# Attention with an adjacency bias: projections in quarters over all steps, checks in the last groups, first loads from two engines

## The chip, the cores and the metric

One Trainium2 chip, one of its cores. The time is device microseconds for one execution of the kernel, the median of several runs; lower is better. The core has a matrix engine (PE), a vector engine (DVE), a scalar engine that does the exponentials (ACT), a general engine (POOL) and a queue engine (SP) that here issues nearly all transfers.

## The reference

The input is `x` (2708 nodes, 128 features), an adjacency matrix `adj` (2708 x 2708, float32), and the weights of two layers. Layer 0 is attention over all pairs of nodes, for 128 "heads" `d` that have 8 features each:

```python
q = (x @ Wq.T).reshape(d, n, h)          # d = 128, n = 2708, h = 8; k and v alike
a = jnp.einsum('dnh,dmh->dnm', q, k) * scale
a = jax.nn.softmax(a + adj + adj, axis=2)
out = jnp.einsum('dnm,dmh->dnh', a, v).reshape(n, h * d) @ Wo.T
x = layernorm(x + out)
```

Layer 1 is two products with `adj`, small weight products and another layernorm. Nearly all the work is in layer 0: 128 x 2708 x 2708 scores, an exponential of each, and the weighted sums.

## The kernel before, in words

**Tiling.** Heads go in 32 groups of four (GB). In a group, queries go in six blocks of 452 (QB; the last has 448), keys in 21 chunks of 128 nodes and a short one of 20. For a block of queries, the pairs (chunk, head) make pieces of two, and one `interleave` step holds two to four pieces: 9 steps per block, 54 per group, 1728 in all. The plan of nine steps is the same for all blocks.

**What a step does.** For each piece, PE multiplies keys and queries into one of two PSUM buffers `s` (`score`, L415), and DVE adds the adjacency columns to it and writes it to the step's tile `e` (`add_near`, L422). ACT then takes exp(2 x) of the whole tile (L518). Nine chunks, one per step (`TWO_EXP`), are treated in another way to relieve DVE: three of their four heads are scored into a PSUM tile `p`, ACT takes exp(2 p) (L515), and POOL multiplies by exp(2 adj) of that chunk (L516). Tiles of products (`w`) and of exponentials (`e`) go to the second product, `add_up` on PE (L440), as moving operands. ACT's order in a step is L515, then L518.

**exp(2 adj).** It is made in group 0, one tile `ecol` per step, by `first_exp` on ACT (L397), just ahead of L515, and stored to `near_exp` in device memory by SP (L398, `ne<-ecol`). Later groups load it. `look_at_near` (L404) reduces such a tile on DVE to a minimum or maximum per row; `rest` tests these, together with the sums, and if a limit is passed a second, slower attention runs. It doesn't run on these inputs.

**The projections.** q, k and v of the first two chunks of 128 rows of `x` are made at the start (L371 to L380), which is what group 0 needs. The other 20 chunks are cut into 120 halves of 512 columns (`halves`), in the order of chunk, then keys, queries, values, then half. A half is one matmul into an `s` buffer (L343), a scaling copy by DVE (L345) and *jobs*. For keys and queries these are a cast and a subtraction on POOL (L356, L357), which split the value into two parts, and a store (L352); for values a store (L347). The last job of each is the load of the next half's weights (`load_half`, L335). `proj` has one buffer for each tile. One job is popped per step, at its second piece:

```python
if c == 1 and jobs:
    jobs.pop(0)()
```

**What sets the order.** `interleave` is a planner: it holds assumed costs (`PROJECT`, `TAKE`, `SPLIT` for projections) and yields pieces, `add_up`s, `amid` (a projection, ahead of the first piece of a step named in `amid`) and `hand_on`. PE gets its instructions in that order, and every engine takes its own in order. SP's queue is in the order of the program too: at the head of a step query loads, key loads and value loads for the next group, adjacency loads eight ahead, then, in group 0, the store of exp(2 adj), and behind it, at the second piece, the job of that step.

**The start.** SP loads `x` and weights, eight adjacency tiles and the first weights of a half; PE, ACT and DVE make the first projections; SP stores keys and queries, loads the 16 parts of `k_raw` (L254) and the eight of `q` (L287), then stores and loads values. The casts of the keys (L262) on POOL, DVE and ACT need all 16 parts.

Of the kernel before, what the change touches and what calls it, by code (L numbers as in the profile page):

```python
# [9 lines left out]
F32 = mybir.dt.float32  # L10
F32R = mybir.dt.float32r
I32 = mybir.dt.int32
AF = mybir.ActivationFunctionType
ALU = mybir.AluOpType
AX = mybir.AxisListType
# [3 lines left out]
P = 128  # L19
H = 8  # L20
GB = 4
NB = 512
# [17 lines left out]
def interleave(plan, blocks, short, amid=(), bufs=4, patience=0.1):  # L40
# [9 lines left out]
    EXP, EXP_ADDED, EXP_TILE = 0.07, 0.14, 0.37  # L50
    PROJECT, TAKE, SPLIT = 0.95, 0.7, 1.25
    n_plan = len(plan)
# [11 lines left out]
    ready, summed, queue, sums, again = {}, {}, [], None, False  # L64
    n, c, left = 0, 0, None
    amid, seen = set(amid), 0
    while n < blocks * n_plan or queue:
# [3 lines left out]
        elif n < blocks * n_plan:  # L71
# [5 lines left out]
            if None not in old:  # L77
                at = added[-2] + HOP
                rows = [r for m, j in tiles for r in (range(GB) if m == short else [j])]
                beside = [j for j in left if j not in rows][:2] if banks + HOP <= max(pe, at) else []  # L80
                if c == len(pieces) - 1:
                    beside = list(left)
                    at = max(at, banks + HOP) if left else at
                starts.append((at, "piece"))
        if queue and not (queue[0][1] == first_chunk and sums is not None):
            qb, qm = queue[0]
            at = max([ready[p, qb * n_plan + k] for p, k in held[qm]] + [free_acc] * (qm == first_chunk)) + HOP
            starts.append((at, "add_up"))
        soon = [s for s in starts if s[0] <= pe + patience]
        at, what = soon[0] if soon else min(starts)  # L90
# [52 lines left out]
def graph_attention_gcn(ctx: ExitStack, tc: tile.TileContext, x, xT, adj, adjT, adjP, adjS,  # L143
# [10 lines left out]
    nc = tc.nc  # L154
# [34 lines left out]
    with ExitStack() as s:  # L189
# [57 lines left out]

        def load_keys(g, h):


            if h == 0:
                groups[g] = kpool.tile([P, NU, P], F32R, tag="k", name="k"), k_short[g % 2], vals[g % 2], v_short[g % 2]
                raw_keys[g] = raw.tile([P, N], F32R, tag="k_raw", name="k_raw")
            nc.sync.dma_start(raw_keys[g][ds(H * h, H), :].bitcast(F32),  # L254
                              ks[ds(H * (h % 4 // 2), H), ds((GB * g + h // 4) * N, N)])
# [25 lines left out]

        def load_q(g, b):
            n0, nw = QBS[b]
            q = queries[g, b] = qpool.tile([P, QB], F32R, tag="q", name="q")
            for j in range(GB):
                for i in range(2):
                    nc.sync.dma_start(q[ds(32 * j + 2 * H * i, 2 * H), :nw].bitcast(F32),  # L287
                                      qs[:, ds((GB * g + j) * N + n0, nw)])
# [31 lines left out]
        assert GB * N <= FIRST * P * P  # L320
        halves = [(c, i, h) for c in range(FIRST, NM) for i in range(3) for h in range(2)]
        given = {}
# [4 lines left out]

        def load_half(n):
            c, i, h = halves[n]
            i0, mi = MC[c]  # L330
            if i == h == 0:
                given[c] = proj.tile([P, P], F32, tag="xc", name="xc")
                nc.sync.dma_start(given[c][:, :mi], xT[:, ds(i0, mi)])
            given[c, i, h] = proj.tile([P, NB], F32, tag="wc", name="wc")
            nc.sync.dma_start(given[c, i, h], projections[i][0][:, ts(h, NB)])  # L335

        def project(n):

            c, i, h = halves[n]
            i0, mi = MC[c]  # L340
            dst = projections[i][1]
            pp = ps.tile([P, 2, NB], F32, tag="s", name="s")
            nc.tensor.matmul(pp[:mi, 0, :], given[c][:, :mi], given.pop((c, i, h)), start=True, stop=True)  # L343
            a = proj.tile([P, NB], F32, tag="pa", name="pa")[:mi]
            nc.vector.tensor_scalar_mul(a, pp[:mi, 0], half_scale if i == 1 else 1.0)  # L345
            if i == 2:
                return [lambda: nc.sync.dma_start(dst.rearrange("(i g) e -> i (g e)", g=P)[ds(i0, mi), ts(h, NB)], a)]  # L347
            o = proj.tile([P, 2, NB], F32R, tag="pr", name="pr")[:mi]

            def store():  # L350
                for l in range(2):
                    nc.sync.dma_start(dst.rearrange("r (i g) -> i r g", g=P)[ds(i0, mi), ds(H * l + 4 * h, 4)],  # L352
                                      o[:, l].bitcast(F32).rearrange("p (e g) -> p e g", g=P))


            return [lambda: nc.gpsimd.tensor_copy(o[:, 0], a),  # L356
                    lambda: nc.gpsimd.tensor_sub(o[:, 1], a, o[:, 0].bitcast(F32)), store]  # L357

# [5 lines left out]
        for n in range(ahead):  # L364
            load_adj(n)
        load_half(0)
        for i, (_, dst) in enumerate(projections):
            for c in range(FIRST):
                pp = ps.tile([P, 2, NB], F32, tag="s", name="s")
                for h in range(2):  # L370
                    nc.tensor.matmul(pp[:, h, :], first_x[:, ts(c, P)], first_w[:, ts(2 * i + h, NB)], start=True, stop=True)  # L371
                o = flat(epool.tile([P, 8, QB], F32, tag="e", name="e"))[:, : 4 * NB].rearrange("p (l f) -> p l f", l=2)
                if i == 2:
                    nc.scalar.copy(o[:, 0], flat(pp))
                    nc.sync.dma_start(dst.rearrange("(i g) e -> i (g e)", g=P)[ts(c, P)], o[:, 0])
                else:
                    f = half_scale if i == 1 else 1.0
                    nc.scalar.mul(o[:, 0].bitcast(F32R), flat(pp), f)
                    nc.vector.scalar_tensor_tensor(o[:, 1].bitcast(F32R), flat(pp), f, o[:, 0], ALU.mult, ALU.subtract)
                    nc.sync.dma_start(dst.rearrange("r (i g) -> i r g", g=P)[ts(c, P)],  # L380
                                      o.rearrange("p l (e g) -> p (l e) g", g=P))
            if i == 1:
                for h in range(16):
                    load_keys(0, h)
                load_q(0, 0)
        for j in range(GB):
# [6 lines left out]
        def first_exp(b, m):  # L393

            nw = QBS[b][1]
            t = ecols.tile([P, QB], F32, tag="ecol", name="ecol")
            nc.scalar.activation(t[:, :nw], adj_cols[0, b, -1 - m][:, :nw], AF.Exp, scale=2.0)  # L397
            nc.sync.dma_start(near_exp[b, m][:, :nw], t[:, :nw])  # L398
            exp_cols[0, b, m] = t

        def look_at_near(g, b, m):
            x = TWO_EXP.index(m)
            if g < 8 and g % 4 == x % 4:
                nc.vector.tensor_reduce(ends[:, g // 4, ds(b * len(TWO_EXP) + x, 1)], exp_cols[g, b, m][:, : QBS[b][1]],  # L404
                                        AX.X, (ALU.min, ALU.max)[g // 4])

# [44 lines left out]

        amid = list(range(2, 54, 6)) + [54 * g + t for g in range(1, NG) for t in (2, 10, 18, 26)]
        amid = amid[: len(halves)]
        for g in range(1, NG):
            c = (min(NG, g + 2) * GB * N - 1) // (P * P)
            assert c < FIRST or amid[halves.index((c, 2, 1))] + 8 < 54 * g
        jobs = []
        loaded = ahead
        for what, n, c, beside in interleave(plan, len(steps) // len(plan), NU, amid, bufs=5):
            if what == "amid":  # L460
                at = amid.index(n)
                jobs += project(at)
                if at + 1 < len(halves):
                    jobs.append(lambda n=at + 1: load_half(n))
                continue
# [368 lines left out]
```

## Time and profile before

| what | value |
|---|---|
| median of 3 runs | 6898.54 us (6897.92 to 6901.11) |
| the profiled execution | 6904.39 us, span of its instructions 6902.6 us |
| start to first exp of products (L515) | 48.7 us |
| group 0, 54 steps | 238.9 us |
| groups 1 to 7 | 202.7 to 208.3 us each |
| groups 8 to 27 | 201.7 to 202.1 us each |
| groups 28 to 31 | 201.2, 199.8, 200.2, 196.7 us |
| the rest (output projection, layer 1) | 346.4 us |
| granted PE clock, mean | 0.994 |

A stage's time is read from one group's first L515 to the next one's. In a row of busy times by stage the number after the window is its length, and for each engine the busy time and the instructions in it follow. In a row of a group of instructions the numbers after "x" are count, busy time, mean nanoseconds of one, and the idle time of the engine just before them with what ended it. In a timeline the first number is the start, the second the duration, and the bracket holds the idle time before and what ended it. Idle time of an engine matters only where ACT, or whatever sets the pace, waits for it.

### The profile page before, as it was taken

Reading aid. Unit: us, or ns where it says so; the run is one execution under the profiler, and the core shown is the slowest. Engines: PE = TensorE matmul, PEld = TensorE weight load, DVE = VectorE, ACT = ScalarE, POOL = GpSimd, SP = SyncE. Lnnn points to the kernel's source line nnn. Section 1 sums busy time; section 2 is a strip of 40 time slices with the busy share of each in tenths; the row PEclk is TensorE's granted clock in tenths of the full one; section 3 lists DMA queues with packets and bytes.
Section 4 is the critical chain, followed back from the end, with each engine's and each line's share of the span. In section 5 each row is a group of like instructions: output and inputs, shape, how many; then the busy total and the mean of one; then the engine's idle time right before and its main releaser. Section 6 shows DMA issues by size and latency. Waiting matters only on the chain.

```text
span 6902.6 us, 137500 instructions
## 1 busy us (share of the span) xinstructions
PE 6641.2 (96%) x50426; PEld 1983.7 (29%) x50426; DVE 6112.2 (89%) x6307; ACT 6501.8 (94%) x3605; POOL 5761.7 (83%) x2546
## 2 busy tenths in 40 slices
PE   7999999999999999999999999999999999999979
PEld 2222222222222222222222222222222222222254
DVE  6899999999999999999999999999999999999941
ACT  7999999999999999999999999999999999999910
POOL 5888888888888989888898988889898888888800
PEclk8999999999999999999999999999999999999999
DMA  8888887878888888888878788877888887777667
GB/s 266 269 246 243 249 239 234 246 241 242 249 245 243 243 246 245 253 246 247 241 242 249 245 251 248 248 240 243 244 244 255 247 240 232 231 235 239 199 203 232
DMA packets 1143258, 1674.16 MB, mean 243 GB/s; under 512 B 148922, under 2 KB 1090366, under 8 KB 1138478
## 3 DMA queue, kind: packets, MB, share of 16 engines
q1 hardware_dynamic: 1142574, 1665.29, 79.7%
q8 instruction: 399, 6.54, 0.4%
q14 instruction: 285, 2.33, 0.1%
HBM read 1582.90 MB, written 81.80 MB: 241 GB/s over the span
## 4 chain that ended last, share of the span: by engine, by line
PE 54%; DMA 13%; DVE 12%; POOL 8%; issue 6%; ACT 4%; SPq 3%; DVEq 0%; POOLq 0%; ACTq 0%
PE acc L440 27%; PE s L415 18%; DVE e L422 11%; POOL w L516 7%; DMA col<-in_adjP 4%; PE acc L661 3%; ACT w L515 2%; DMA k_raw<-ks 2%; PE p L415 2%; ACT e L518 2%; PE acc L437 2%; DMA two<-in_adjP 2%; DMA ecol<-ne 1%; PE s L343 1%; DMA q<-qs 1%
## 5 line engine op out<-in xcount | busy, mean ns | idle before, releaser
L516 POOL TENSOR_TENSOR w<-w,ecol 128x1356 f32<-128x1356 f32 (+1 forms) x1728 | 5347.4, 3102 | 755.0 <-ACT w L515 622.6
L422 DVE TENSOR_TENSOR e<-s,col 128x904 f32<-128x904 f32 (+1 forms) x4608 | 4831.3, 1092 | 339.9 <-PE s L415 196.8
L518 ACT ACTIVATE e<-e 128x2712 f32<-128x2712 f32 (+5 forms) x1728 | 4747.6, 2747 | 17.4 <-DVE e L422 14.8
L440 PE MATMUL acc<-e,vals 128*9 128x452 f32 x20352 | 3553.2, 545 | 0.1
L415 PE MATMUL s<-q,k 32*128 32x452 f32 x10944 | 2501.3, 462 | 183.4 <-DVE e L422 117.7
L515 ACT ACTIVATE w<-p 128x1356 f32<-128x1356 f32 (+1 forms) x1728 | 2439.2, 1412 | 47.1 <-PE p L415 28.5
L415 PEld LDWEIGHTS s<-q,k 32*128 32x128 f32 x10944 | 1016.7, 182 | 3370.6 <-DVE e L422 2979.4
L440 PE MATMUL acc<-w,vals 128*9 128x452 f32 x10368 | 1622.6, 545 | 0.0
L415 PE MATMUL p<-q,k 32*128 32x452 f32 (+1 forms) x5184 | 1400.5, 446 | 18.7 <-ACT w L515 18.4
L422 DVE TENSOR_TENSOR e<-s,two 128x904 f32<-128x904 f32 (+1 forms) x960 | 1049.1, 1093 | 119.9 <-PE s L415 61.1
L440 PEld LDWEIGHTS acc<-e,vals 128*9 128x9 f32 x20352 | 452.0, 89 | 807.7 <-issue 805.8
L415 PEld LDWEIGHTS p<-q,k 32*128 32x128 f32 x5184 | 575.5, 182 | 63.9 <-ACT w L515 53.6
L440 PEld LDWEIGHTS acc<-w,vals 128*9 128x9 f32 x10368 | 200.9, 88 | 193.2 <-issue 177.5
L262 POOL CAST k<-k_raw 128x336 fp32r<-128x336 f32 x251 | 222.3, 886 | 37.6 <-DMA q<-qs 37.6
L432 PE MATMUL acc<-e,v_short 128*128 128x452 f32 (+1 forms) x384 | 197.1, 595 | 0.0
L437 PE MATMUL acc<-e,v_first 128*32 128x452 f32 (+1 forms) x1536 | 185.9, 556 | 2.5
L343 PE MATMUL s<-wc,xc 128*128 128x512 f32 (+1 forms) x240 | 136.3, 650 | 6.4 <-DMA wc<-in_WvT 3.4
L345 DVE TENSOR_SCALAR pa<-s 128x512 f32<-128x512 f32 (+1 forms) x120 | 82.9, 691 | 48.6 <-PE s L343 46.2
L446 DVE COPY o<-acc 128x452 f32<-128x452 f32 x192 | 118.9, 619 | 6.4 <-PE acc L440 6.4
L661 PE MATMUL acc<-col,xw 128*128 128x512 f32 (+2 forms) x264 | 105.5, 549 | 0.0
L555 ACT ACTIVATE sd<-mv,eps 128x1 f32<-128x1 f32 (+1 forms) x22 | 6.0, 294 | 104.5 <-DVE mv L549 104.4
L661 PE MATMUL acc<-col,hw 128*128 128x512 f32 (+2 forms) x264 | 104.1, 545 | 0.0
(84 smaller groups left out, 1069.0 us busy)
## 6 DMA issues: line engine op xcount, KB each, us to landing
col<-in_adjP SPq DMA_DIRECT2D x1965, 226.0 KB
two<-in_adjP SPq DMA_DIRECT2D x1440, 226.0 KB
ecol<-ne SPq DMA_DIRECT2D x1395, 226.0 KB
col<-in_adjP SPq DMA_DIRECT2D x393, 224.0 KB
two<-in_adjP SPq DMA_DIRECT2D x288, 224.0 KB
ecol<-ne SPq DMA_DIRECT2D x279, 224.0 KB
col<-in_adjT SPq DMA_DIRECT2D x210, 256.0 KB
k_raw<-ks SPq DMA_DIRECT2D x512, 84.6 KB
```

The source lines that it names most:

```text
L262: copy(k[:, :, ts(i, n)], t[:, ts(i, n * NU)].rearrange("p (q c) -> p c q", c=NU))
L343: nc.tensor.matmul(pp[:mi, 0, :], given[c][:, :mi], given.pop((c, i, h)), start=True, stop=True)
L415: nc.tensor.matmul(to[:, :nw], k[r, m, :], q[r], start=True, stop=True)
L422: nc.vector.tensor_add(e[:, ds(at, 2), :nw], st[:, :, :nw], a)
L432: nc.tensor.matmul(a[:, :nw], vz, e[:, t, :nw], start=False, stop=False)
L437: nc.tensor.matmul(a[ds(32 * j, 32), :nw], v_first[g % 2][:, ds(32 * j, 32)], e[:, t, :nw], start=True, stop=False)
L440: nc.tensor.matmul(a[ds(32 * j, VW), :nw], v[:, m, ds(VW * j, VW)], e[:, t, :nw], start=False, stop=(m == last_chunk))
L446: nc.vector.tensor_copy(o[:, :nw], acc.pop((g, b))[:, :nw])
L515: nc.scalar.activation(w[:, :, :nw], sp[:, :, :nw], AF.Exp, scale=2.0)
L516: nc.gpsimd.tensor_mul(w[:, :, :nw], w[:, :, :nw], exp_cols[g, b, two][:, :nw].unsqueeze(1).to_broadcast([P, 3, nw]))
L518: nc.scalar.activation(e[:, :at, :nw], e[:, :at, :nw], AF.Exp, scale=2.0)
L661: nc.tensor.matmul(acc[:, :nw], src[:mw, m, :], t[:mw, :nw], start=(m == 0), stop=(last is None and m == NM - 1))
```

## The change

Three things change.

1. Projections are cut in quarters of 256 columns instead of halves of 512: 240 instead of 120. Before, the steps of `amid` were nine in group 0 (every sixth from 2) and four in each later group (2, 10, 18, 26) until they were used up in group 28. Now they are 18 in group 0 (every third from 2), and then every seventh step from 58 to 1605, in group 29. Cast and subtraction are one job, so that keys and queries have three jobs (split, store, load the next) and values two (store, load the next). The planner's costs of a projection are lowered.
2. The check of exp(2 adj): the maximum is replaced by the row sum that `first_exp` leaves as accumulator output, in group 0. The minimum is taken in groups 29 to 31, three of the nine chunks in each, instead of minima in groups 0 to 3 and maxima in groups 4 to 7: 54 reductions instead of 108.
3. At the start, query stores, every third part of the keys and half of the query parts are issued by ACT instead of SP. The loads of keys and queries are written after all first projections, and the value stores behind them, so SP's own order of these is as before.

```diff
-    PROJECT, TAKE, SPLIT = 0.95, 0.7, 1.25
+    PROJECT, TAKE, SPLIT = 0.5, 0.36, 1.0
...
-        halves = [(c, i, h) for c in range(FIRST, NM) for i in range(3) for h in range(2)]
+        quarters = [(c, i, h) for c in range(FIRST, NM) for i in range(3) for h in range(4)]
+        QW = 2 * P
...
-            nc.tensor.matmul(pp[:mi, 0, :], given[c][:, :mi], given.pop((c, i, h)), start=True, stop=True)
-            a = proj.tile([P, NB], F32, tag="pa", name="pa")[:mi]
-            nc.vector.tensor_scalar_mul(a, pp[:mi, 0], half_scale if i == 1 else 1.0)
+            nc.tensor.matmul(pp[:mi, 0, :QW], given[c][:, :mi], given.pop((c, i, h)), start=True, stop=True)
+            a = proj.tile([P, QW], F32, tag="pa", name="pa")[:mi]
+            nc.vector.tensor_scalar_mul(a, pp[:mi, 0, :QW], half_scale if i == 1 else 1.0)
+
+            def load():
+                if n + 1 < len(quarters):
+                    load_quarter(n + 1)
+
             if i == 2:
-                return [lambda: nc.sync.dma_start(dst.rearrange("(i g) e -> i (g e)", g=P)[ds(i0, mi), ts(h, NB)], a)]
+                to = dst.rearrange("(i g) e -> i (g e)", g=P)[ds(i0, mi), ts(h, QW)]
+                return [lambda: nc.sync.dma_start(to, a), load]
...
+            def split():
+
+                nc.gpsimd.tensor_copy(o[:, 0], a)
+                nc.gpsimd.tensor_sub(o[:, 1], a, o[:, 0].bitcast(F32))
...
-            return [lambda: nc.gpsimd.tensor_copy(o[:, 0], a),
-                    lambda: nc.gpsimd.tensor_sub(o[:, 1], a, o[:, 0].bitcast(F32)), store]
+            return [split, store, load]
...
-                    nc.sync.dma_start(dst.rearrange("r (i g) -> i r g", g=P)[ts(c, P)],
-                                      o.rearrange("p l (e g) -> p (l e) g", g=P))
-            if i == 1:
-                for h in range(16):
-                    load_keys(0, h)
-                load_q(0, 0)
+                if i == 2:
+                    made[c] = o
+                else:
+                    (nc.sync if i == 0 else nc.scalar).dma_start(dst.rearrange("r (i g) -> i r g", g=P)[ts(c, P)],
+                                                                 o.rearrange("p l (e g) -> p (l e) g", g=P))
+        for h in range(16):
+            load_keys(0, h, nc.scalar if h % 3 == 2 else nc.sync)
+        load_q(0, 0, (nc.sync, nc.scalar))
+        for c in range(FIRST):
+            nc.sync.dma_start(vs.rearrange("(i g) e -> i (g e)", g=P)[ts(c, P)], made[c][:, 0])
...
-            nc.scalar.activation(t[:, :nw], adj_cols[0, b, -1 - m][:, :nw], AF.Exp, scale=2.0)
+            x = b * len(TWO_EXP) + TWO_EXP.index(m)
+            nc.scalar.activation(t[:, :nw], adj_cols[0, b, -1 - m][:, :nw], AF.Exp, scale=2.0,
+                                 accum_out=ends[:, 1, x : x + 1])
...
-            if g < 8 and g % 4 == x % 4:
-                nc.vector.tensor_reduce(ends[:, g // 4, ds(b * len(TWO_EXP) + x, 1)], exp_cols[g, b, m][:, : QBS[b][1]],
-                                        AX.X, (ALU.min, ALU.max)[g // 4])
+            if x % 3 == g - NG + 3:
+                nc.vector.tensor_reduce(ends[:, 0, ds(b * len(TWO_EXP) + x, 1)], exp_cols[g, b, m][:, : QBS[b][1]],
+                                        AX.X, ALU.min)
...
-        amid = list(range(2, 54, 6)) + [54 * g + t for g in range(1, NG) for t in (2, 10, 18, 26)]
-        amid = amid[: len(halves)]
+        amid = list(range(2, 54, 3))
+        amid += range(58, 58 + 7 * (len(quarters) - len(amid)), 7)
...
                 jobs += project(at)
-                if at + 1 < len(halves):
-                    jobs.append(lambda n=at + 1: load_half(n))
```

## The prediction

> **What bounds the kernel now.** First the page's busy shares and its slices, then the busy time by stage with one stage per group of four heads, then the groups by form for prices, and last the timeline at the start and at one projection.
>
> ```profile
> PE 6641.2 (96%) x50426; PEld 1983.7 (29%) x50426; DVE 6112.2 (89%) x6307; ACT 6501.8 (94%) x3605; POOL 5761.7 (83%) x2546
> ```
>
> No engine stands out over the whole span, so I cut it. A stage runs from the first exp of products (L515 on ACT) of one group to that of the next, 54 steps:
>
> ```profile
> core 0: us, PE busy (x) PEld busy (x) DVE busy (x) ACT busy (x) POOL busy (x), PEclk, DMA share, GB/s
> 48.68:287.53 238.85, 212.83 (x1498) 59.06 (x1502) 199.15 (x208) 226.61 (x161) 188.30 (x92) 0.95 0.90 276
> 490.44:698.74 208.30, 198.84 (x1542) 55.73 (x1538) 191.67 (x197) 202.52 (x110) 181.10 (x81) 0.98 0.79 238
> 1109.43:1312.13 202.70, 198.26 (x1548) 56.33 (x1540) 192.09 (x198) 200.84 (x109) 180.64 (x81) 1.00 0.81 244
> 2125.71:2327.42 201.71, 197.85 (x1542) 56.11 (x1538) 186.06 (x185) 200.43 (x110) 179.21 (x79) 1.00 0.81 245
> 5959.52:6159.30 199.78, 192.99 (x1534) 57.44 (x1530) 182.02 (x180) 199.78 (x110) 175.26 (x75) 1.00 0.77 233
> ```
>
> In group 29 (last row), which has neither projections nor checks, ACT is busy for all of its 199.78 us: ACT sets the pace, and a step costs 3.7 us. Groups 8 to 27 have four half projections each and take 201.7 to 202.1: 1.7 us for four. Groups 1 to 7 have the same halves and 12 or 18 checks each, and take 1434.65 together, 22.6 more than seven times 201.72: 0.25 us for each of 90 checks. Group 0 takes 238.85: the floor of 199.8, plus 54 exps of the adjacency (L397) on ACT that lengthen a step by 0.47 each (25.4), plus about 13 of idle ACT. So the whole that can be won from projections and checks is their sum over the groups, some 80 us, and nothing that only frees DVE or PE wins unless ACT was waiting for it.
>
> ```profile
> L397 ACT ACTIVATE ecol<-col 128x452 f32<-128x452 f32 x45 | 26.2, 583 | 0.0
> L404 DVE TENSOR_REDUCE ends<-ecol 128x1 f32<-128x452 f32 x90 | 55.4, 616 | 6.2 <-ACT ecol L397 6.2
> L343 PE MATMUL s<-wc,xc 128*128 128x512 f32 x228 | 130.1, 653 | 6.4 <-DMA wc<-in_WvT 3.4 <-DMA wc<-in_WkT 2.2 <-DVE e L422 0.7
> L345 DVE TENSOR_SCALAR pa<-s 128x512 f32<-128x512 f32 x114 | 78.8, 691 | 47.4 <-PE s L343 45.6 <-POOL w L516 1.3
> ```
>
> The third row is the one to keep: the projection's matmul has already waited for its weights (wc), 3.4 and 2.2 us, both in group 0. The timeline shows what one such wait costs:
>
> ```profile
> 155.91 0.35 SPq L335 DMA_DIRECT2D wc<-in_WvT  x1
> 157.62 1.31 ACT L515 ACTIVATE w<-p 128x1356 f32<-128x1356 f32 x1
> ...
> 160.68 1.24 PE L343 MATMUL s<-wc,xc 128*128 128x512 f32 x2 [3.36 <-DMA wc<-in_WvT]
> 162.03 0.69 DVE L345 TENSOR_SCALAR pa<-s 128x512 f32<-128x512 f32 x1 [3.91 <-PE s L343]
> 167.67 1.30 ACT L515 ACTIVATE w<-p 128x1356 f32<-128x1356 f32 x1 [5.17 <-PE p L415]
> ```
>
> PE takes its work in order, so everything behind the projection waits too. ACT's L515 comes 10.05 us after the one before instead of about 4.7: 5.3 us lost by a 3.36 us wait. The rest is the clock: from 161.5 to 168.3 PEclk is 0.50 and score matmuls take about 740 ns instead of 470.
>
> At the start, the 16 key loads and 8 query loads set the first score:
>
> ```profile
> 20.97 13.79 SPq L254 DMA_DIRECT2D k_raw<-ks  x16
> 35.45 7.07 SPq L287 DMA_DIRECT2D q<-qs  x8
> 42.33 1.68 ACT L262 CAST k<-k_raw 128x336 fp32r<-128x336 f32 x2 [20.55 <-DMA q<-qs]
> ```
>
> **What the Trainium skill says.** "TensorE: Matmul & The Clock Gate", Part 1, has the array fall to half its clock after an idle window of about 3.4 us; the trace agrees, with half clock for 6.8 us after the wait of 3.36. "DMA: Bandwidth & Descriptors", Issuing engines are not separate DMA queues, says that transfers of all issuing engines interleave on the same 16 DMA engines and only issue time is saved; its section Why a DMA increments its semaphore by 16 and not by 1 says that a transfer of 8 partitions uses the lowest 8 of them. The trace agrees with the second: during the key loads (26.5 to 36 us) the DMA share is 0.51, at 89 GB/s, one load per 0.96 us. "ScalarE: Activation LUTs", What ACT_TABLE_LOAD costs, prices a ScalarE instruction at 186 ns plus 0.833 per element, with 93 of overlap; I use it for an accumulator read below, which this trace doesn't contain.
>
> **The change part by part.** A(n) is the start of L515 of step n.
>
> *Late loads in group 0.* Before, halves come every 6 steps; for keys and queries the jobs are cast, subtract, store, load, one per step, so the next weights are asked for at step n+3 and used at n+6. Now a quarter comes every 3 steps, jobs are split, store, load: asked for at n+2, used at the head of n+3. On SP's queue this load stands right behind the store of exp(2 adj) of step n+2 (ne<-ecol), which waits for that step's L397, done 0.12 us after A(n+2) (ACT's in-order queue puts it just ahead of L515). So the load can't be issued before A(n+2)+0.12+0.35 (that store's issue)+0.1. It then lands after 2.27 us (the v_raw load issued at 45.31, when the queue was idle, released POOL at 47.58) and 0.66 more for the store's 226 KB ahead of it at 340 GB/s: A(n+2)+3.5. PE wants it earlier: in the eight later halves of group 0 it came to the projection 0.1 to 2.3 us, on average 1.3, before the A of the step just finished. Wait: 3.5+1.3 = 4.8 us. A wait of 3.36 with 6.8 us of half clock and a lead of 0.3 cost 5.3; a wait of 2.2 at step 44 with 3.4 us of half clock and a lead of 0.9 cost 3.0. Both fit wait, plus about a third of the half-clock time, less lead. Here 4.8, plus 1.1 to 2.3, less 1.3: about 5.0. Of the 17 loads inside group 0, 13 follow a key or query quarter: +65. The other four follow a value quarter, asked for one step earlier, land about when wanted: +4. If SP runs late, as it did before (the load at 155.91 stood 7 us after its step's A), it is more; but stalls give the DMA queues time, which at 0.90 share they lacked. Low end 1.5 each (+20), high 8 (+104). What group 0's halves and checks cost before goes: the idle ACT beyond the first two steps' fill, -10.7.
>
> *Accumulator output on L397.* No instruction is added in the program; the chip may add a read of one element. Bounds: 0, and 0.29 (the one-element sqrt, L555, has mean 295 ns), on 54 steps of an engine that is the bound there. By the skill's price, less overlap, 0.1: +5.5 (0 to +16).
>
> *Checks.* 18 in group 0 (inside the -10.7) and 90 in groups 1 to 7 go: -22.6. 54 come back in groups 29 to 31, on DVE behind a step's last addition, so that the next step's first scores wait for their buffer. They cost 0.25 in groups with halves; without, ACT's lead over the last p there is 0.35 to 1.55 us, so take 0.2: +11 (0 to +15).
>
> *Quarters in groups 1 to 29.* 222 instead of 111. PE: a half is about 1.13 us, a quarter half of that and a new fill, 0.62 (estimate): 7.7 a group make 4.8 instead of 4.5. DVE: 691 ns at 512 and 620 for a 452-wide copy from PSUM give 1.2 ns per element, so 0.39 instead of 0.69. Of four halves two cost nothing and two 0.7 and 1.1, by the lead of the step they fall on. A quarter delays by some 0.7, lead is 0.35 to 1.5: about 0.2 on average, 1.5 a group as now. Saving in groups 8 to 27: about -3; groups 28 and 29 get quarters they lacked: +2. Ends: nothing lost (-32), or as much per quarter as per half (+48). Their own jobs are covered: weights have four steps, POOL's split of 1.15 instead of 1.91 us stands in idle time of 0.6 per step, except in steps 33 to 49, where key casts (886 ns each) leave it little.
>
> *Two issuers.* Query stores move behind ACT's L378, delaying only value copies that wait for nothing near; key loads may start while query stores (to 25.4 us) still run, about 2.5 us earlier, and two rings on the same 8 engines may overlap a little: -4 (0 to -9). If the later casts had no ACT free, nothing.
>
> Sum: -4 +65 +4 -10.7 +5.5 -22.6 +11 -3 +2 = +47. The profiled execution took 6904.4 (span 6902.6), the median is 6898.5, so 5.9 below: 6951.6 and 6945.7. I say 6945.
>
> **The rivals.** *Loads land in time* (15 in 100): transfers of half the size land sooner, or PE's lead vanishes once it has stalled. Then group 0 saves 8, and the rest stands: -4-8+5.5-22.6+11-1 = -19, 6879. It decides at about 1.5 us per late load, where 13 of them eat the gain. Against it: SP's order and ACT's order, which no lead can go round. *Quarters cost as halves do* (12): short lead at i = 0, 2 and 8 catches each; on top of the forecast +48, 6993. For it: the leads of 0.35; against: lead recovers within a step or two. *Quarters cost nothing* with late loads (12): +47-32, 6914. *SP stays late* (6): 8 us per load, 6985. *The startup or the checks decide alone* has no room: together under 40 us.
>
> **How the numbers follow.** Forecast 55 in 100, its own range 6920 to 6970. 0.2% (14 us) is about what a measurement of this kernel can tell from no change. Faster: most of the first rival, 0.13. Same: the cheap quarters and mild stalls, 0.12. Slower: 0.75. Eight in ten from 6882 to 6992.
>
> **What would show it.** In the profile after, the stage of group 0 should be 290 to 315 us, with waits of the quarter's matmul on wc of 3 to 6 us, 13 or so, PEclk there below 0.9, ACT's L515 waiting for p. Groups 1 to 7 should each be near 201.7, as 8 to 28; groups 29 to 31 some 3 to 4 longer than before. First L515 at 40 to 48. A group 0 of 235 would make the prediction wrong; so would groups at 200 or at 203.5.

## The result and the profile after

The changed kernel takes 6990.8 us (median of 4 runs, 6986.2 to 6995.8) against 6899.8 us (4 runs, 6897.9 to 6905.5): a ratio of 1.0131, 95% interval 1.0113 to 1.0148. It is 91 us slower, about twice the 46 that were forecast. The profiled execution of the changed kernel has a span of 6984.4 us, 81.8 above that of before; what follows adds up to these 81.8, and the last 9 come from how far each profiled execution lies from its median.

The page's busy shares after:

```profile
PE 6676.5 (96%) x50666; PEld 1999.7 (29%) x50666; DVE 6106.2 (87%) x6373; ACT 6507.5 (93%) x3659; POOL 5787.2 (83%) x2706
```

Busy time hardly moved: ACT has 5.7 us more, DVE 6.0 less, PE 35.3 more. A span that grew by 82 us with engines this little busier has grown by waiting. The busy time by stage says where. Its columns are those of the view shown for before; the rows are group 0, group 5, group 10, group 18 and group 29:

```profile
core 0: us, PE busy (x) PEld busy (x) DVE busy (x) ACT busy (x) POOL busy (x), PEclk, DMA share, GB/s
48.08:400.61 352.53, 237.00 (x1536) 65.23 (x1536) 192.08 (x199) 233.87 (x214) 190.65 (x102) 0.78 0.65 192
1205.35:1406.37 201.02, 197.79 (x1550) 56.82 (x1546) 186.31 (x189) 200.67 (x110) 182.95 (x89) 1.00 0.82 248
2210.07:2410.79 200.72, 197.59 (x1554) 56.89 (x1546) 186.17 (x189) 200.57 (x109) 181.03 (x85) 1.00 0.83 250
3818.13:4024.29 206.16, 200.33 (x1553) 56.89 (x1546) 186.55 (x189) 201.05 (x110) 179.86 (x83) 0.98 0.79 238
6035.04:6238.88 203.84, 197.66 (x1538) 55.15 (x1534) 193.59 (x204) 201.34 (x109) 177.71 (x79) 1.00 0.77 236
```

Group 0 took 352.53 us instead of 238.85, with ACT busy for 233.87 of it. Everything else together became shorter. By stage, before and after, with the forecast's share of the sum beside it:

| stage | before, us | after, us | change | forecast |
|---|---|---|---|---|
| start to first L515 / L530 | 48.7 | 48.1 | -0.6 | -4 |
| group 0 | 238.85 | 352.53 | +113.7 | +64 |
| groups 1 to 7 | 1434.65 | 1407.70 | -27.0 | -22.6 |
| groups 8 to 28 | 4237.34 | 4226.72 | -10.6 | -2 |
| groups 29 to 31 | 596.64 | 604.46 | +7.8 | +12 |
| the rest | 346.45 | 344.90 | -1.6 | 0 |

Group 18, at 206.16, is an outlier of that one execution. At 3869.8 us DVE waited 2.82 us for an adjacency load, 4 us after a stretch of 6 us in which the DMA queues moved only 88 GB/s, and PE then ran at half clock. Why the queues were slow there stays open. In the four profiled experiments below that keep all three parts of the change and load weights early enough, group 18 took 200.9 to 201.0.

The chain of group 0 is in its waits. The waits of the changed kernel from 48.08 to 400.61 us, with columns total us, times, longest us:

```profile
PEld s L344 <- issue: 113.5, 15, 11.4
DVE pa L346 <- PE s L344: 113.1, 18, 11.4
ACT w L530 <- PE p L432: 84.5, 12, 11.0
PE s L344 <- DMA wc<-in_WqT: 47.5, 6, 11.0
PE s L344 <- DMA wc<-in_WkT: 45.3, 7, 9.4
PE s L344 <- DMA wc<-in_WvT: 14.8, 4, 6.7
```

The last three rows are the same event in all 17 quarters whose weights were asked for inside group 0: 107.6 us in which PE stands at the head of its queue with a projection, until the weights have landed. The third row is what ACT sees of it: the products `p`, queued behind that projection, come late. (Line numbers moved: L530 is before's L515, L344 its L343, L346 its L345, L412 its L397, L421 its L404.)

The longest of these waits, in the timeline, with start and duration first and the idle time before in brackets:

```profile
119.76 1.30 ACT L530 ACTIVATE w<-p 128x1356 f32<-128x1356 f32 x1 [6.72 <-PE p L432]
120.48 1.39 SPq L465 DMA_DIRECT2D os<-o  x4
121.97 4.51 SPq L287 DMA_DIRECT2D q<-qs  x8
...
128.59 1.28 ACT L530 ACTIVATE w<-p 128x1356 f32<-128x1356 f32 x1
128.76 0.38 SPq L414 DMA_DIRECT2D ne<-ecol  x1
129.24 1.00 SPq L364 DMA_DIRECT2D ks<-pr  x2
130.33 1.68 SPq L303 DMA_DIRECT2D col<-in_adjP  x3
132.12 0.57 ACT L412 ACTIVATE ecol<-col 128x452 f32<-128x452 f32 x1
132.48 0.33 SPq L414 DMA_DIRECT2D ne<-ecol  x1
...
132.91 0.38 SPq L336 DMA_DIRECT2D wc<-in_WqT  x1
...
138.26 1.19 PE L344 MATMUL s<-wc,xc 128*128 128x256 f32 x2 [11.02 <-DMA wc<-in_WqT]
139.56 0.42 DVE L346 TENSOR_SCALAR pa<-s 128x256 f32<-128x256 f32 x1 [11.39 <-PE s L344]
...
143.75 1.30 ACT L530 ACTIVATE w<-p 128x1356 f32<-128x1356 f32 x1 [10.97 <-PE p L432]
```

L530 at 128.59 is A(13) in the prediction's terms. The forecast had the store of that step's exp(2 adj) at A + 0.12 and the weights' load at A + 0.57. SP came to that store at 132.48, A + 3.89 and so 3.77 late, because it had spent 120.48 to 126.48 on four `os` stores and eight query loads and then had a step's worth of other issues in front. The load left at 132.91 and landed 5.35 us later, where the forecast had 2.93. PE had been ready since 127.24. So the wait of 11.02 is 1.35 of lead, 4.32 to the issue and 5.35 to the landing.

The rows of the groups by form that answer to those of before:

```profile
L344 PE MATMUL s<-wc,xc 128*128 128x256 f32 x456 | 167.2, 450 | 109.2 <-DMA wc<-in_WqT 47.5 <-DMA wc<-in_WkT 45.3 <-DMA wc<-in_WvT 14.8
L346 DVE TENSOR_SCALAR pa<-s 128x256 f32<-128x256 f32 x228 | 95.2, 418 | 127.8 <-PE s L344 126.9 <-POOL w L531 0.4
L421 DVE TENSOR_REDUCE ends<-ecol 128x1 f32<-128x452 f32 x45 | 27.5, 612 | 0.0
L412 ACT ACTIVATE ecol<-col 128x452 f32<-128x452 f32 x45 | 25.6, 568 | 0.0
L412 ACT ACTIVATION_READ_ACCUMULATOR ecol<-col 128x1 f32 x54 | 10.3, 191 | 0.0
```

The last row is new: the accumulator output is an instruction of its own on ACT, 191 ns on each of the 54 tiles. About half of that shows: an undisturbed step of group 0 took 4.01 us before and takes 4.10 now.

The timeline at the start shows both engines issuing:

```profile
17.26 19.37 SPq L254 DMA_DIRECT2D k_raw<-ks  x11
18.45 2.76 ACTq L393 DMA_DIRECT2D qs<-e  x1
21.41 5.60 ACTq L254 DMA_DIRECT2D k_raw<-ks  x1
27.04 6.16 ACTq L254 DMA_DIRECT2D k_raw<-ks  x4
33.66 1.80 ACTq L287 DMA_DIRECT2D q<-qs  x4
36.67 3.36 SPq L287 DMA_DIRECT2D q<-qs  x4
41.69 1.68 ACT L262 CAST k<-k_raw 128x336 fp32r<-128x336 f32 x2 [18.46 <-DMA q<-qs]
```

SP's eleven key loads now take 19.37 us to issue, where all sixteen took 13.79 before, and the cast begins at 41.69 instead of 42.33.

### The profile page after: what moved, and what is told of

The parts are those of the page before. It is cut to its first block, busy times and chain, and to the rows that moved or that the text cites. A ratio compares the mean times of both kernels' runs of the same rounds, so it can differ in the third digit from the quotient of the medians.

```text
span 6984.4 us, 138831 instructions
## 1 busy us (share of the span) xinstructions
PE 6676.5 (96%) x50666; PEld 1999.7 (29%) x50666; DVE 6106.2 (87%) x6373; ACT 6507.5 (93%) x3659; POOL 5787.2 (83%) x2706
## 4 chain that ended last, share of the span: by engine, by line
PE 62%; DVE 11%; DMA 10%; issue 5%; ACT 5%; SPq 3%; POOL 2%; DVEq 0%; ACTq 0%; POOLq 0%
PE acc L457 32%; PE s L432 20%; DVE e L439 10%; DMA col<-in_adjP 3%; ACT e L533 3%; PE acc L676 3%; DMA two<-in_adjP 3%; PE p L432 2%; POOL w L531 2%; PE acc L449 2%; ACT w L530 2%; SPq L287 2%; PE s L344 2%; PE s L429 1%; DMA ot<-os 1%
## 5 line engine op out<-in xcount | busy, mean ns | idle before, releaser
L533 ACT ACTIVATE e<-e 128x2712 f32<-128x2712 f32 (+5 forms) x1728 | 4573.1, 2646 | 30.8 <-DVE e L439 26.0
L530 ACT ACTIVATE w<-p 128x1356 f32<-128x1356 f32 (+1 forms) x1728 | 2263.2, 1310 | 111.0 <-PE p L432 92.4
L432 PE MATMUL p<-q,k 32*128 32x452 f32 (+1 forms) x5184 | 1328.4, 444 | 3.8 <-ACT w L530 1.3
L432 PEld LDWEIGHTS p<-q,k 32*128 32x128 f32 x5184 | 551.5, 183 | 24.7 <-ACT w L530 21.3
L344 PE MATMUL s<-wc,xc 128*128 128x256 f32 (+1 forms) x480 | 174.5, 447 | 109.7 <-DMA wc<-in_WqT 47.5
L346 DVE TENSOR_SCALAR pa<-s 128x256 f32<-128x256 f32 (+1 forms) x240 | 100.1, 417 | 128.1 <-PE s L344 126.9
L344 PEld LDWEIGHTS s<-wc,xc 128*128 128x128 f32 (+1 forms) x480 | 72.7, 191 | 230.3 <-issue 119.8
L360 POOL TENSOR_TENSOR pr<-pa,pr 128x256 fp32r<-128x256 f32 (+1 forms) x160 | 117.6, 735 | 12.8
```

The source lines that it names most:

```text
L344: nc.tensor.matmul(pp[:mi, 0, :QW], given[c][:, :mi], given.pop((c, i, h)), start=True, stop=True)
L432: nc.tensor.matmul(to[:, :nw], k[r, m, :], q[r], start=True, stop=True)
L530: nc.scalar.activation(w[:, :, :nw], sp[:, :, :nw], AF.Exp, scale=2.0)
L533: nc.scalar.activation(e[:, :at, :nw], e[:, :at, :nw], AF.Exp, scale=2.0)
```

## The experiments

The theory after the result: all of group 0's loss is the weights' load, which is asked for too late, stands behind other work in SP's queue, and lands slowly; the other parts of the change do about what was forecast. The rivals are that the quarters themselves, their number or their place in every third step, cost this, or the accumulator output, or the start.

**The load asked for first.** This is the changed kernel with one difference: the next quarter's load is the first job instead of the last, two steps earlier for keys and queries.

```diff
-                return [lambda: nc.sync.dma_start(to, a), load]
+                return [load, lambda: nc.sync.dma_start(to, a)]
...
-            return [split, store, load]
+            return [load, split, store]
```

> The changed kernel with one thing undone in effect: the load of the next quarter's weights is the first job of a projection instead of its last, so it is asked for at step n and not at n+2, two steps (8 us) earlier; split and store come one step later. Theory (weights asked for too late): the waits of the quarter's matmul on wc, 107 us in group 0 of the changed kernel, fall to under 15 us; group 0 takes 236 to 250 us instead of 352.5, and the whole 6876 to 6892 us, below the kernel before. Rival (quarters every third step are too dense for PE, DVE and POOL in group 0, whatever the loads do): group 0 stays above 300 us, the whole above 6935.

Measured: 6882.0 us, ratio to the kernel before 0.9974 (0.9965 to 0.9983). Group 0 by stage:

```profile
core 0: us, PE busy (x) PEld busy (x) DVE busy (x) ACT busy (x) POOL busy (x), PEclk, DMA share, GB/s
46.20:294.75 248.55, 222.85 (x1540) 62.66 (x1544) 193.07 (x200) 231.91 (x214) 188.92 (x101) 0.90 0.87 264
```

The same quarters, in the same steps, with the same accumulator output: group 0 falls from 352.53 to 248.55 us, waits on `wc` from 107.6 to 5.2, and the whole is faster than the kernel before. PE's busy time falls from 237.00 to 222.85 for the same work, and its granted clock rises from 0.78 to 0.90: beside the waits PE loses time to half clock. The theory holds, and the rivals of quarters and accumulator fall as causes of the loss.

**The kernel before with late loads.** The reverse: halves as before, but in group 0 each half's load is put off, so that it is asked for one step before its use instead of three (behind keys and queries) or five (behind values).

```diff
-                    jobs.append(lambda n=at + 1: load_half(n))
+                    jobs += [lambda: None] * (5 - len(jobs)) * (at < 8) + [lambda n=at + 1: load_half(n)]
```

> The kernel before with its halves, in group 0 alone the load of the next half's weights two steps later for keys and queries (three or four for values), so that it is asked for one step ahead of its use, as in the changed kernel. Nothing else is changed. Theory (late weights): eight halves wait 5 to 10 us each as the quarters do, by the place in the nine steps (about 5 at i = 8, 10 at i = 5, 6 at i = 2), group 0 goes from 239 to 285 to 305 us, the whole to 6945 to 6965. Rival (the density of quarters): group 0 stays within 10 us of 239, the whole within 10 us of 6900.

Measured: 6971.2 us, ratio 1.0106 (1.0085 to 1.0126). Group 0 by stage:

```profile
44.11:356.07 311.96, 229.33 (x1498) 61.89 (x1502) 200.43 (x208) 227.25 (x162) 188.25 (x92) 0.83 0.71 211
```

Group 0 took 311.96 us, and the whole 6971.2, both above the expected ranges. Its waits on `wc` are 68.2 us in 8 loads, 8.5 each. So late loads alone, with none of the change, make 73 of the 114 us that group 0 lost. The quarters waited 6.3 us each, but that these loads of 256 KB were waited for longer than the quarters' 128 KB isn't shown to come from their size: they landed 4.7 us after their issue, against 4.4 for the quarters, and SP issued four of the eight only 4.0 to 5.3 us after the last A before their use.

**The checks alone.** The kernel before with only the second part of the change (accumulator output, 54 minima in the last three groups).

```diff
-            nc.scalar.activation(t[:, :nw], adj_cols[0, b, -1 - m][:, :nw], AF.Exp, scale=2.0)
+            x = b * len(TWO_EXP) + TWO_EXP.index(m)
+            nc.scalar.activation(t[:, :nw], adj_cols[0, b, -1 - m][:, :nw], AF.Exp, scale=2.0,
+                                 accum_out=ends[:, 1, x : x + 1])
...
-            if g < 8 and g % 4 == x % 4:
+            if x % 3 == g - NG + 3:
```

> The kernel before with the change of the checks alone: row sums as accumulator output in group 0, 54 minima in groups 29 to 31, none in groups 0 to 7. Theory: groups 1 to 7 save about 22, the accumulator reads cost 54 times 0.09 = 5, groups 29 to 31 lose 6 to 11: the whole 6 to 12 us faster, near 6890. Rival (the gain of groups 1 to 7 in the changed kernel came from smaller projections and not from the checks): groups 1 to 7 stay near 204.9 each, the whole 5 to 15 us slower than before.

Measured: 6888.6 us, ratio 0.9982 (0.9975 to 0.9989). Groups 1 to 7 took 1412.00 us instead of 1434.65, a saving of 22.65; groups 29 to 31 took 603.82 instead of 596.64, a cost of 7.2; group 0 took 240.86, 2.0 more. So the saving of groups 1 to 7 is that of the checks, and this part alone is a small gain.

**Query loads a step earlier.** The changed kernel with the next block's query loads at step i = 2 of the nine instead of i = 3, in group 0. The longest waits were at i = 5; if they come from the eight query loads in front of them, they shrink.

```diff
-                if i == 3 and nq[0] < NG:
+                if i == (2 if g == 0 else 3) and nq[0] < NG:
```

> The changed kernel with the eight query loads of a block issued at step i = 2 of the nine instead of i = 3, in group 0 alone. In the changed kernel SP was 2.3 to 4.3 us behind ACT where a quarter's weights are asked for at i = 4, right behind those loads, and the waits of the quarters at i = 5 were 9 to 11 us instead of 5 to 7. Theory (what stands ahead of the load on SP's queue makes up the difference): these five or six waits fall by 2 to 4 us each, group 0 by 8 to 25 us to about 330 to 344. Rival (the long waits at i = 5 come from something else, as the length of that step): they stay at 9 to 11, group 0 within 5 us of 352.

Measured, in one execution: 6968.4 us, group 0 336.53. The waits at i = 5 after the first block fell from 11.0, 10.2, 9.4 and 9.5 us to 6.3, 4.4, 7.1 and 6.2, and the sum on `wc` from 107.6 to 88.1. So SP's lateness behind the query loads is part of the wait, and 16 us of group 0's loss. The quarter at i = 5 behind a value quarter also fell, from 6.7 to 2.2; the other places kept theirs to within 1.3 us.

**The start alone.** The kernel before with only the third part of the change.

```diff
-            nc.sync.dma_start(raw_keys[g][ds(H * h, H), :].bitcast(F32),
+            queue.dma_start(raw_keys[g][ds(H * h, H), :].bitcast(F32),
...
-            if i == 1:
-                for h in range(16):
-                    load_keys(0, h)
-                load_q(0, 0)
+        for h in range(16):
+            load_keys(0, h, nc.scalar if h % 3 == 2 else nc.sync)
+        load_q(0, 0, (nc.sync, nc.scalar))
```

> The kernel before with the change of the start alone: query stores, a third of the key parts and half of the query parts issued by ACT. Theory (the eight DMA engines that the key loads use are the limit, not the issue): the first exp of products comes at most 1 us earlier than in the kernel before on the same footing, the whole within 3 us of it, which can't be told from no change. Rival (issue was the limit, as the prediction's 4 us had it in part): 4 to 9 us faster, and the key packets end 4 us or more before the 41.1 us of the kernel before.

Measured in 13 runs: 6904.2 us, ratio 1.0007 (0.9999 to 1.0015); the first L515 came at 48.3 us instead of 48.7. No change can be told.

**Weights two quarters ahead.** As the first experiment, with two buffers for weights and for the chunk of `x`, and loads two quarters ahead.

```diff
-            given[c, i, h] = proj.tile([P, QW], F32, tag="wc", name="wc")
+            given[c, i, h] = proj.tile([P, QW], F32, tag="wc", name="wc", bufs=2)
...
-                if n + 1 < len(quarters):
-                    load_quarter(n + 1)
+                if n + 2 < len(quarters):
+                    load_quarter(n + 2)
```

> The first experiment's kernel with weights loaded two quarters ahead (two buffers for weights and for x), so that a load has five steps or more. Theory: the waits left over in it (3.2 us at step 26, 1.8 at step 20) go too, and with them half-clock time; group 0 takes 236 to 244 us instead of 248.5, the whole 6872 to 6880 us. Rival (what is left in group 0 is not from loads): group 0 stays at 247 to 250.

Measured: 6880.1 us, ratio 0.9967 (0.9955 to 0.9980). All waits on `wc` are gone, and group 0 still took 250.54, next to the 247 to 250 of this run's rival: taking away the last 5 us of waits on weights gained nothing that shows. Its waits in group 0 name another tile of the same pool:

```profile
DVE pa L346 <- DMA vs<-pa: 10.1, 3, 4.9
POOL pr L359 <- DMA qs<-pr: 2.4, 1, 2.4
```

DVE's copy of a quarter waits until the values of an earlier one have been stored, because `pa` has one buffer and its store stands late in SP's queue. While it waits, the projection holds one of the two score buffers. The first experiment had 8.6 us of these waits too.

**Halves, the load first.** The kernel before, with only the order of the jobs changed.

```diff
-                jobs += project(at)
+                todo = project(at)
                 if at + 1 < len(halves):
                     jobs.append(lambda n=at + 1: load_half(n))
+                jobs += todo
```

> The kernel before with only the order of jobs changed: the load of the next half's weights first, three steps earlier for keys and queries, one for values. Theory: the two waits of the kernel before (3.4 us at step 26, 2.2 at step 44) go, with the 8.3 us that ACT lost there; group 0 takes 228 to 233 us instead of 239, the whole 6 to 10 us less. Rival (those losses have other causes): group 0 stays within 3 us of 239.

Measured in 13 runs: 6896.3 us, ratio 0.9993 (0.9984 to 1.0001), not told from no change. Group 0 of the profiled execution:

```profile
45.07:279.00 233.93, 215.60 (x1498) 59.81 (x1502) 199.44 (x208) 226.57 (x162) 188.32 (x92) 0.94 0.90 280
```

That is 4.9 less, with no wait on `wc` left, and just above the 228 to 233 expected. The size fits the 5.6 us of waits that before had there, and not the 8.3 that the prediction ascribed to them; the total can't confirm it.

**The load at the head of the step.** The changed kernel, with the load issued at the head of the step after the store job, ahead of that step's adjacency loads and of its store of exp(2 adj), and not behind them. It is later than in the first experiment, but it doesn't stand behind that step's store.

```diff
+            if c == 0 and n in due:
+                due.pop(n)()
```

> The changed kernel with the load of the next weights moved on SP's queue by most of one step: from behind step n+2's adjacency loads and its store of exp(2 adj) to the head of that step, ahead of them. The wait of SP on that step's exp on ACT (L412) no longer holds the load. Theory: it is issued at about A(n+1)+0.5, lands some 4.4 us later and is wanted 1.3 us before A(n+2): waits of 1 to 3 us where SP is on time and 3 to 5 where it is late, 30 to 55 us in all instead of 107; group 0 takes 270 to 305 us. Rival (landing itself, and not the place in the queue, sets the wait): waits stay at 5 to 9, group 0 above 330.

Measured, in one execution: 6916.6 us, group 0 285.27. Waits on `wc` are 48.4 us in 12 loads:

```profile
PE s L344 <- DMA wc<-in_WqT: 24.2, 6, 7.6
PE s L344 <- DMA wc<-in_WkT: 22.2, 5, 8.4
PE s L344 <- DMA wc<-in_WvT: 2.0, 1, 2.0
```

Group 0 and the waits are within the expected ranges. It is the same step on paper, and the place in SP's queue within it is worth 67 us of the 104 that asking for the weights first gives back.

**Two buffers for the copy and its split form.** As the run with weights two quarters ahead, with a second buffer for `pa` and `pr`.

```diff
-            a = proj.tile([P, QW], F32, tag="pa", name="pa")[:mi]
+            a = proj.tile([P, QW], F32, tag="pa", name="pa", bufs=2)[:mi]
...
-            o = proj.tile([P, 2, QW], F32R, tag="pr", name="pr")[:mi]
+            o = proj.tile([P, 2, QW], F32R, tag="pr", name="pr", bufs=2)[:mi]
```

> The run with weights two quarters ahead, and two buffers instead of one for the scaled copy of a quarter (pa) and for its split form (pr). In the run without them, group 0 still took 250.5 us, and DVE's copy waited 10.1 us in three places on a store of values (vs<-pa), and POOL's split 2.4 us in one on a store of queries (qs<-pr), because the tile was still being stored. Theory: these waits are most of what group 0 has left over its floor of 199.8 + 25.4 + 4.9 and the fill of its first steps; group 0 takes 242 to 246 us, waits of L346 on vs<-pa are gone, the rest is as it was, 6868 to 6876 us in all. Rival: what is left comes from half clock and adjacency loads, and group 0 stays at 249 to 252, 6877 to 6884.

Measured: 6871.1 us, ratio 0.9953 (0.9937 to 0.9970), with the run after it the fastest of all. Group 0:

```profile
core 0: us, PE busy (x) PEld busy (x) DVE busy (x) ACT busy (x) POOL busy (x), PEclk, DMA share, GB/s
50.05:290.31 240.26, 219.44 (x1540) 62.08 (x1544) 194.11 (x200) 231.25 (x214) 188.75 (x100) 0.93 0.88 272
```

240.26 us is 10.3 less than without the buffers and below the 242 to 246 expected; waits of L346 on `vs<-pa` are gone. The theory of this run holds for the profiled execution; of the totals, 6868 to 6876 us here and 6874 to 6882 without the buffers, the ranges just overlap. It is also the base for what follows: group 0 with this change and with no late load in it.

**The same, with query loads a step earlier.**

> As the run with two buffers for copy and split form, and in group 0 the query loads of the next block at step i = 2 of its nine instead of i = 3. In the runs of this study the losses that group 0 keeps fall on the step after i = 5, where SP is still behind by what it issued at i = 3 and 4. Theory: group 0 gains 2 to 5 us on the run with two buffers alone. Rival: with no wait on weights, copy or split form left, SP's lateness reaches nobody, and group 0 is within 1.5 us of that run.

Measured: 6871.9 us, ratio 0.9954 (0.9937 to 0.9970); group 0 took 243.20. This is 2.9 more than the run it is compared with, outside both expectations, while the totals are 0.8 apart with runs that span 2 to 8 us. No gain is shown. Nor is it shown that SP's lateness reaches nobody: what the two group 0 differ by goes with the clock, which has a mean of 0.90 here against 0.93, and most of ACT's idle time still falls on the steps after i = 5.

## Why the prediction was right and wrong

The direction, the mechanism and its place were right: group 0, the quarter's matmul waiting on `wc`, PEclk below 0.9, ACT waiting for `p`, each of the other stages within 9 us. The size was not. The step that failed is *Late loads in group 0*: its "+65" for 13 loads "about 5.0 each". Their waits were 7.4 us on average instead of 4.8, because both the time to the issue and the time from issue to landing were put too low. Together the other stages took 15 us less than forecast, which hid a part of the miss.

**What the term measured.** Over those 13 loads, from the trace after, in means, with the prediction's own split of the wait ("i = 5" are the loads for a quarter at step i = 5 of the nine):

| part of the wait | forecast, us | 13 loads | the 5 at i = 5 | the other 8 |
|---|---|---|---|---|
| A of the step to the issue of the load | 0.57 | 1.80 | 3.63 | 0.66 |
| issue to landing | 2.93 | 4.36 | 4.79 | 4.08 |
| PE ready ahead of A | 1.3 | 1.25 | 1.43 | 1.14 |
| wait | 4.8 | 7.41 | 9.85 | 5.88 |

PE's lead was right. The landing was taken from a load on an idle queue (2.27 us, plus 0.66 for the store ahead of it). Two of the 13, used at 177.08 and 348.63, did land 2.89 and 3.09 us after their issue, as forecast; the other eleven took 4.07 to 5.35. The difference goes with what else is on its way. For those two the DMA engines moved 311 to 314 KB of other transfers between the load's issue and its own last packet, for the eleven 600 to 1311 KB. So the forecast counted one store of 226 KB and left out the other transfers, most of them adjacency loads, that SP asks for around it. The load at 132.91 and the first of the two quick ones, from issue to use, with the columns of the busy times by stage (the last two are DMA share and GB/s):

```profile
132.91:138.26 5.35, 0.00 (x1) 0.03 (x1) 0.00 (x0) 0.00 (x0) 0.09 (x1) 0.50 1.04 295
174.19:177.08 2.89, 0.00 (x0) 0.03 (x1) 0.00 (x0) 2.89 (x4) 2.08 (x1) 0.50 0.71 187
```

A number for a busy moment was in the prediction's own fence: the load issued at 155.91 was used at 160.68, 4.77 us later. The issue time followed SP's order in the program but supposed that SP is at that step on time. The load for a quarter at i = 5 is asked for at i = 4, right behind the eight query loads of i = 3, and there it isn't. The prediction knew the case ("the load at 155.91 stood 7 us after its step's A") and put it into its low and high ends and into the rival *SP stays late* instead of into the forecast. That rival, given 6 in 100 and 8 us per load, is near the mean of the 13 but gives them all one cause: SP is late for five of them, and the slow landing concerns eleven. That its total, 6985, is 6 us from the measured one is in part luck, since the other stages took less than forecast.

**From wait to loss.** The forecast's rule, a loss of 5.0 for a wait of 4.8, was right. Against the 240.26 us of group 0 with no late load, the changed kernel lost 112.3 us for 107.6 of waits; the run with the load at the head of the step 45.0 for 48.4; and halves with late loads, against 233.93 with the load first, 78.0 for 68.2. So ACT loses 0.9 to 1.15 us per us that PE waits: about what the lead saves, half clock takes back.

**The four loads behind value quarters**, "+4", waited 1.11, 6.67, 0.47 and 3.05 us, 11.3 together. The 6.67 is at i = 5 too. At the same rate that is some 12 us, so this term was too small as well.

**What group 0's halves and checks cost before, "-10.7".** With it group 0 without late loads should have taken 238.85 - 10.7 + 5.5 = 233.7; the best run has 240.26. So 6.6 of it didn't come. Two runs price what was to go: before's own waits on weights 4.9 (halves with the load first), and the 18 checks 2.9 (the checks alone added 4.9 of accumulator to group 0 and left it 2.0 longer). The rest was not theirs, or eighteen quarters cost more there than nine halves: halves with the load first and the checks changed would take 233.93 + 2.0 = 235.9 (an estimate from those two runs), 4.3 less than the best run. ACT is still idle for 9.0 us in the best run's group 0. Of these, 1.5 are in the first two steps, which the forecast left in, and 5.6 in the step after i = 5 of three blocks. In each of the three PE goes to half clock, at 149.73, 190.69 and 231.65 us, although no weights are waited for. Why PE was idle enough for that just there stays open. Together, 112.3 - 69 = 43.3 and 6.6 make the 50 us by which group 0 passed its forecast of +64.

**Accumulator output, "+5.5".** 0.09 us on 54 steps, 4.9. The price of the Trainium skill, "ScalarE: Activation LUTs", What ACT_TABLE_LOAD costs, 186 ns less 93 of overlap, fits the 191 ns and the 0.09 us measured. It was in part luck: the page gives it for an activation, and the accumulator read turned out to be an instruction of its own.

**Checks, "-22.6" and "+11".** -22.65 and +7.2 in the run with the checks alone: a reduction at the end costs 0.13 us, not 0.2.

**Quarters in groups 1 to 29, "-3" and "+2".** They are cheaper than that. Groups 8 to 28 took 10.6 us less, or 13.7 less in the best run, whose execution has no outlier like group 18; groups 1 to 7 gained 4 to 5 us beyond the checks. A group's 7.7 quarters cost some 1.2 us over the floor of 199.8, so 0.16 each instead of 0.2. Both rivals on this term, at no cost and at the cost of halves, fall: a group takes 201.0, not 200 and not 203.5.

**Two issuers, "-4".** Nothing that can be told, as the start alone showed. The casts began 0.6 us earlier, not 4.

**Loads land in time**, the rival on the other side, was wrong for the kernel as it is: PE's lead didn't vanish (1.25 us), and the loads landed later than forecast, not sooner. Its number is what comes when the loads do land in time: with the load asked for two steps earlier the kernel takes 6882.0 us, 0.26% less than before, close to the 6879 that this rival gave.

## What to carry to other kernels

A transfer that is asked for one step before its use is priced by where its issue stands in its queue, by what that queue is late with at just that step, and by its landing behind the bytes that the queue issued just before it; a landing time from an idle moment is a lower bound. When a piece of work is cut finer, count the steps between asking and using again, since halving the interval here took the slack from three steps to one, and ask for the next input before the jobs that dispose of the last output. A single-buffered staging tile whose store is late holds its producer, and through it a scarce PSUM buffer: it is the next wait once the input is early.

## What was not expected of the hardware

PE falls to half clock with no long idle stretch before it. In the kernel before, around 127 us, the busy time by stage reads

```profile
core 0: us, PE busy (x) PEld busy (x) DVE busy (x) ACT busy (x) POOL busy (x), PEclk, DMA share, GB/s
121.00:124.00 3.00, 2.96 (x22) 1.00 (x18) 1.84 (x3) 3.00 (x3) 2.35 (x1) 1.00 0.97 283
124.00:127.30 3.30, 1.88 (x23) 0.50 (x15) 3.30 (x4) 3.30 (x3) 2.28 (x1) 1.00 1.08 361
127.30:130.60 3.30, 3.30 (x22) 0.73 (x18) 2.67 (x4) 3.30 (x3) 2.38 (x2) 0.51 1.06 320
```

In the 3.3 us ahead of the half clock PE was busy for 1.88, and its longest waits there were 0.89 and 0.53 us. The Trainium skill, "TensorE: Matmul & The Clock Gate", Part 1, has the clock fall after an idle window of about 3.4 us; here a stretch in which PE was busy for 57% was enough. Nor was PE idle all through at the wait of 3.36 us that the prediction took as agreeing: it was busy for 0.83 of the 3.41 us before that fall, from 158.10 to 161.51. A share of 57% is no threshold either: in the changed kernel PE was busy for 1.89 of the 3.41 us from 87.93 us on, 55%, and the clock stayed full for the next 3.41. What the clock does look at stays open here. The stretches of half clock last whole multiples of one length: of those that begin inside group 0, the three before lasted 3.41 or 6.83 us, and the sixteen after 3.41, 6.83, 10.24 or 13.65.

Two issuing engines did raise the rate at which the keys came: from 26.5 to 36 us the queues moved 149 GB/s instead of 89 at about the same DMA share (0.53 and 0.51). But the casts needed the last of them, and that came only 0.6 us earlier. The start itself varies by more than that: among the profiled runs here the first exp of products came at 44.1 to 50.1 us.
